# A fused cross-attention and Fourier FFN kernel: copies of weights on other engines or through score banks, a mask and norms ahead of reciprocals, transposes inside a chain

## The chip, the cores and the metric

The kernel runs on one core of a Trainium2 chip. A core has five engines with queues of their own that run in the order in which the program issues to each: TensorE (PE, matrix products and transposes, with weight loads shown apart as PEld), VectorE (DVE), ScalarE (ACT), GpSimd (POOL) and SyncE (SP, here only a queue that starts DMAs). They meet through semaphores. The metric is the device time of one execution in microseconds. The time before is a median over three runs; the profile is one further execution.

## The reference

The inputs are x (2 x 2048 x 512), an encoder context (2 x 128 x 512), and a mask that is 0 for valid keys and 1 for padded ones; all is float32.

```
xn    = layernorm(x)
q,k,v = xn @ wq + bq, ctx @ wk + bk, ctx @ wv + bv          # 16 heads of 32
score = (q k^T / sqrt(32)) * mask;  score = -1e9 where score == 0
x     = x + concat(softmax(score) v) @ wo + bo
x     = x + real(ifft(fft(layernorm(x)) @ (w_re + i w_im))) + bias
```

The FFN's transforms and its weight are all linear, so the kernel works out one real 512 x 512 matrix first (m_ffn), from DFT tables that come in as constants, and the FFN of a row is then one product with it.

## The kernel before, in words

The 4096 rows are cut into eight groups of 512 (i = 0 to 7), each into four tiles of 128 rows (t = 0 to 3). One pass (i, t) computes the scores of one tile against the 128 keys for 16 heads, as two halves w[0] and w[1] of eight heads; `begin(i, t)` issues the 32 score matmuls. Each half goes through four steps of class `Softmax`:

- `masked`: DVE multiplies the scores, in PSUM, with the mask (L345);
- `maxima`: DVE turns zeros into the large negative value and takes a minimum per head (L352, L354, L355);
- `exponentials`: ACT, eight activations with their sums (L361);
- `divided`: DVE takes a reciprocal of the sums (L373) and POOL multiplies by it (L374).

`transposed_weights(i, t, first, end, eng, banks)` then turns the heads' weights on PE, four heads to a bank of PSUM (tpw, L391), and copies the bank to SBUF (pt), on DVE (L396) or ACT (L398). Each bank needs both halves of its tile. Four such banks make a tile, and they are issued as two pairs.

Around the passes other work is laid out by hand. Order in the source is order in each engine's queue. For each group: rows come in by DMA; `relative` subtracts the row's first element (L244, mostly on POOL), `query_statistics` has DVE's statistics (L219, L220) and two POOL steps for the inverse deviation (L223, L224), `query_norm` normalises on DVE (L227), and `query_transposes` turns the tile on PE (tp_a, L194) with a copy on ACT (L196). `Queries` is a chain of matmuls with the query weight and an eviction with the bias, on ACT (L307) or DVE (L309). `context` multiplies turned weights with the values (c, L413), `Project` with wo (o, evicted by DVE into the residual rows, L450). Then the FFN follows: `ffn_statistics`, `ffn_norm` (norm_f on DVE, L227, and then on POOL the addition of the FFN's bias to the residual, L469), `ffn_transposes` (tp_f) and `Ffn` (y, L210 by way of `chain`, evicted by DVE, L514, and stored by DMA). `chain` can call other work between its second and third contraction chunk.

Passes of group 0 and the first two of group 1 are written out one by one, since the making of m_ffn lies between them: `First` (chains h, eviction on ACT L669, sums on POOL L677 and L679 in `first`, and on DVE L690 and L691 in `second`) and `Mirrored` (m, L722, evicted by ACT L732 and L738, finished on POOL L739 and L740). From pass (1, 2) on the function `slot` issues a pass. It takes three chains and lists of further work, called at fixed places: `on_a` follows the mask of the second half, `on_m` its maxima, `on_b` the reciprocal of the first half and the eviction of the second chain, `on_c` the end. Work in the list `carried` is called in the next slot, just behind the first half's mask. The last two groups have lists of their own.

PSUM is held in three pools of two: ps_sc (score tiles of two banks), ps_tp (transposes, one bank) and ps_mm (chains, one bank). A tile waits for the readers of the tile that had its place.

Of the kernel before, what the change touches and what calls it, by code (L numbers as in the profile page):

```python
# [9 lines left out]
FP = mybir.dt.float32  # L10
# [4 lines left out]
P = 128  # L15
# [7 lines left out]
def kernel(  # L23
# [34 lines left out]
    nc = tc.nc  # L58

    B, S, D = x.shape  # L60
    K = enc.shape[1]
    DH = 32
    H = D // DH
    NC = D // P
    NR = P // DH
    HH = H // 2
    TG = 4
# [8 lines left out]
    ps_sc = ctx.enter_context(  # L76
        tc.tile_pool(name="ps_sc", bufs=2, space=bass.MemoryType.PSUM)
    )
# [7 lines left out]
    HC = NC // 2  # L86
# [113 lines left out]
    def call(work):  # L200
        for f, *args in work:
            f(*args)
# [31 lines left out]
    def relative(i, t, eng):  # L234


        xt = rows[i][t]
        d = work.tile([P, D], FP, tag="rel", bufs=4, name=f"rel_{i}_{t}")
        if eng is nc.scalar:
            less = small.tile([P, 1], FP, tag="less", name=f"less_{i}_{t}")  # L240
            nc.scalar.mul(less, xt[:, 0:1], -1.0)
            nc.scalar.activation(d, xt, AF.Identity, bias=less)
        else:
            eng.tensor_scalar(d, xt, xt[:, 0:1], None, ALU.subtract)  # L244
        rels.setdefault(i, []).append(d)
# [15 lines left out]
    def query_statistics(i, first, end):  # L261
        if first == 0:
            mv = small.tile([P, TG, 2], FP, tag="mv", name=f"mv_{i}")
            rstd = small.tile([P, TG], FP, tag="rstd", name=f"rstd_{i}")
            stats[i] = mv, rstd
        mv, rstd = stats[i]
        for t in range(first, end):
            statistics(rels[i][t], mv[:, t, :], f"a{i}_{t}")
        if i == 0:
            inverse_deviations(rstd[:, first:end], mv[:, first:end, 1])  # L270
        elif end == TG:
            inverse_deviations(rstd, mv[:, :, 1])

    def query_norm(i, t):
        mv, rstd = stats[i]
        normalize(rels[i][t], rels[i][t], mv[:, t, :], rstd[:, t : t + 1])

    def query_transposes(i, t):
        if t == 0:
            xnTs[i] = big_tile("xnT", 1, f"xnT_{i}")  # L280
        transpose_rows(
            xnTs[i][:, :, t * P : (t + 1) * P], rels[i][t], f"a{i}_{t}", nc.scalar
        )

    class Queries:
# [5 lines left out]
        def pe(self):  # L291
            i, g = self.i, self.g
            if i not in qTs:
                qTs[i] = big_tile("qT", 2, f"qT_{i}")
            self.ps = chain(
                f"q_{i}_{g}",
                lambda c: wq[:, c, g * P : (g + 1) * P],
                lambda c: xnTs[i][:, c, self.first * P :],
                width=GQ - self.first * P,
                spare=self.spare,  # L300
            )
# [76 lines left out]
    pts = {}  # L378

    def transposed_weights(i, t, first, end, eng=None, banks=None):  # L380
        if t == 0 and first == 0:
            pts[i] = [big_tile("pt", 6, f"pt_{i}_{g}") for g in range(NC)]
        ws = weights[i, t]
        for g in range(first, end):
            ps = (
                banks[g]
                if banks
                else ps_tp.tile([P, NR, P], FP, tag="tp", name=f"tpw_{i}_{t}_{g}")
            )
            for r in range(NR):  # L390
                nc.tensor.transpose(  # L391
                    ps[:, r, :], ws[r // 2].w[:, (r % 2) * NC + g, :], ident
                )
            dst = pts[i][g][:, :, t * P : (t + 1) * P]
            if eng:
                eng.tensor_copy(dst, ps)  # L396
            else:
                nc.scalar.copy(dst, ps)  # L398


    cTs = {}
# [231 lines left out]
    class First:  # L633
# [8 lines left out]
            else:  # L642
                self.lhs = [lambda c, t=t: t[:, c, HD + g :: HC] for t in (wi, wr)]

        def pe(self):
            ps = self.ps = ps_mm.tile([P, D], FP, tag="mm", name=self.name)
            at = 0


            for k, table, odd, n in (  # L650
                (0, cosines, 0, QD + 1),
                (0, cosines, 1, QD),
                (1, sines, 0, QD - 1),
                (1, sines, 1, QD),
            ):
                for b in range(2):
                    c = b * HC + odd
                    nc.tensor.matmul(
                        ps[:, at : at + n],
                        self.lhs[k](c),  # L660
                        table[:, c, :n],
                        start=(b == 0),
                        stop=(b == 1),
                    )
                at += n

        def evict(self):
            self.t = work.tile([P, D], FP, tag="parts", name=f"t_{self.name}")
# [73 lines left out]
    carried = []  # L742

    def run(job):
        job.pe()
        job.evict()
# [115 lines left out]
    h = [First(what, g) for what in range(2) for g in range(HC)]  # L862
    m = [Mirrored(f"m_{g}", half_of(g), m_ffn[:, g, :]) for g in range(NC)]
    rest = [Queries(0, g, 1, g >= HC) for g in range(NC)]
    q = [Queries(1, g) for g in range(NC)]
    values = [Values(b) for b in range(B)]

    w = begin(0, 0)
# [22 lines left out]
    w = begin(0, 1)  # L891
    w[0].masked()
    query_transposes(1, 0)
    query_transposes(1, 1)
    for t in range(TG):
        relative(2, t, nc.gpsimd)
    w[0].maxima()
    values[1].pe(between=[(query_transposes, 1, 2), (query_transposes, 1, 3)])
# [6 lines left out]
    w[1].exponentials()  # L905
    h[0].evict()
    w[0].divided()
    q[0].pe()
    transposed_weights(0, 0, HC, NC)
    q[0].evict()  # L910
    query_statistics(2, 0, TG)
    w[1].divided()
    h[0].first()

    load_rows(3)
    w = begin(0, 2)
# [16 lines left out]
    q = [Queries(2, g) for g in range(NC)]  # L933
    w = begin(0, 3)
    w[0].masked()
    query_transposes(2, 0)
    query_transposes(2, 1)
    h[1].pe()
    query_transposes(2, 2)
    query_transposes(2, 3)  # L940
    h[1].evict()
    w[0].maxima()
    h[0].second()
# [25 lines left out]
    w = begin(1, 0)  # L969
# [6 lines left out]
    relative(3, 3, nc.gpsimd)  # L976
    m[1].pe()
    m[1].evict(add[:, 1:2])
    w[0].exponentials()
    w[1].masked()  # L980
    transposed_weights(0, 3, 0, HC, nc.vector)
    w[1].maxima()
    w[0].divided()
    m[2].pe()
# [10 lines left out]
    w = begin(1, 1)  # L995
# [7 lines left out]
    w[0].exponentials()  # L1003
    w[1].masked()
    q[2].evict()
    transposed_weights(1, 0, 0, HC, nc.vector)
    w[1].maxima()
    run(q[3])
    transposed_weights(1, 0, HC, NC)
    w[1].exponentials()  # L1010
    query_norm(3, 0)
    query_norm(3, 1)
    w[0].divided()
    w[1].divided()


    for i in range(1, last - 1):
        p, pp, n, nn = i - 1, i - 2, i + 1, i + 2
        q = [Queries(n, g) for g in range(NC)]
        q_nn = Queries(nn, 0)  # L1020
        o = [Project(p, t) for t in range(TG)]
        f_p = Ffn(p, 0)
        if i > 1:
            load_rows(nn)
            load_mask(n)
            load_residual(p)
            f_pp = [Ffn(pp, t) for t in range(TG)]
            slot(
                i,
                0,  # L1030
                [f_pp[1], f_pp[2], q[1]],
                turned=(p, TG - 1),
                early=[(ffn_transposes, pp, 2)],
                pool=[(relative, nn, t, nc.gpsimd) for t in range(TG)],
                on_b=[(ffn_norm, pp, 3), (query_statistics, nn, 0, 2)],
                on_c=[(query_statistics, nn, 2, TG)],
                end=[(context, p, 0, 2)],
            )
            slot(
                i,  # L1040
                1,
                [q[2], q[3], f_pp[3]],
                turned=(i, 0),
                early=[(context, p, 2, NC), (ffn_transposes, pp, 3)],
                pool=[(output_bias, p)],
                on_b=[(query_norm, nn, 0), (query_norm, nn, 1)],
            )
        slot(
            i,
            2,  # L1050
            o[:3],
            turned=(i, 1),
            early=[(query_transposes, nn, 0), (query_transposes, nn, 1)],
            on_a=[(ffn_statistics, p, 0)],
            on_b=[(ffn_norm, p, 0), (query_norm, nn, 2), (query_norm, nn, 3)],
            on_c=[(ffn_statistics, p, 1)],
            end=[(ffn_transposes, p, 0)],
        )
        slot(
            i,  # L1060
            3,
            [o[3], f_p, q_nn],
            turned=(i, 2),
            early=[(query_transposes, nn, 2), (query_transposes, nn, 3)],
            on_a=[(ffn_statistics, p, 2)],
            on_b=[(ffn_norm, p, 1), (ffn_statistics, p, 3)],
            on_c=[(ffn_norm, p, 2)],
            end=[(ffn_transposes, p, 1)],
        )
# [4 lines left out]
    i, n, p, pp = last - 1, last, last - 2, last - 3  # L1074
    load_mask(n)
    load_residual(p)
    q = [Queries(n, g) for g in range(NC)]
# [9 lines left out]
        on_b=[(ffn_norm, pp, 3)],  # L1087
        end=[(context, p, 0, 2)],
# [16 lines left out]
        on_b=[(ffn_statistics, p, 0)],  # L1105
# [9 lines left out]
        on_b=[(ffn_norm, p, 1), (ffn_statistics, p, 2), (ffn_statistics, p, 3)],  # L1115
        end=[(ffn_transposes, p, 1)],
    )
    i, p, pp = last, last - 1, last - 2
# [14 lines left out]
    w = begin(i, 1)  # L1133
# [19 lines left out]
    w = begin(i, 2)  # L1153
# [22 lines left out]
    w = begin(i, 3)  # L1176
# [93 lines left out]
```

## Time and profile before

| What | Before |
|---|---|
| median of 3 runs | 535.35 us (534.28 to 536.14) |
| the profiled execution | 534.98 us |
| its span, first to last instruction | 533.0 us |
| DMA over the span | 36.49 MB, mean 68 GB/s |
| granted TensorE clock | 1.000 |

The first two are device times; the span is what the trace covers of the profiled one, so 1.98 us lie around it. In a page's row of an engine stand its busy time, its share of the span and its instructions. In a row of the timeline stand start, length, engine, line, operation, tiles, shapes and a count of like instructions in a row; a bracket tells how long the engine was idle before it, and who ended that.

### The profile page before, as it was taken

How to read it: one execution, taken by the hardware profiler on the slowest of the kernel's cores; microseconds unless marked ns; L12 is line 12 of the kernel's file. 1: busy time of each engine (PE TensorE's matmuls, PEld its weight loads, DVE VectorE, ACT ScalarE, POOL GpSimd, SP SyncE). 2: the span in 40 equal slices, each digit the busy share in tenths (PEclk: the TensorE clock that was granted, in tenths of full speed). 3: DMA queues.
4: the chain of work that ended last, by engine and by line, in shares of the span. 5: the costliest groups of instructions: out<-in, count | busy, mean ns of one | idle time of the engine just before them, and what ended most of it. 6: DMA issues, size and time to landing. Idle time of an engine off the chain costs nothing.

```text
span 533.0 us, 8813 instructions
## 1 busy us (share of the span) xinstructions
PE 522.4 (98%) x3028; PEld 293.3 (55%) x3028; DVE 440.6 (83%) x621; ACT 337.5 (63%) x1286; POOL 336.8 (63%) x276
## 2 busy tenths in 40 slices
PE   8999998998999999999999999999999999999997
PEld 7756675554545555455545555455545555455444
DVE  4788799879987998889987999879867899898351
ACT  3367777476677676666677766666686677766210
POOL 2779469844895459735895459825754466856450
PEclk9999999999999999999999999999999999999999
DMA  9962020000610024000510015000311101301102
GB/s 311 387 231 79 1 88 13 1 1 1 199 41 1 21 73 165 1 20 1 198 41 0 22 42 196 1 22 0 119 41 41 59 0 61 100 0 42 39 0 80
DMA packets 22892, 36.49 MB, mean 68 GB/s; under 512 B 2104, under 2 KB 7488, under 8 KB 22848
## 3 DMA queue, kind: packets, MB, share of 16 engines
q1 hardware_dynamic: 22160, 34.75, 18.9%
q10 hardware_dynamic: 688, 1.18, 0.6%
q8 instruction: 24, 0.39, 0.3%
q14 instruction: 20, 0.16, 0.1%
HBM read 27.53 MB, written 8.39 MB: 67 GB/s over the span
## 4 chain that ended last, share of the span: by engine, by line
PE 74%; DVE 17%; ACT 4%; issue 2%; POOL 1%; DMA 1%; SPq 0%; ACTq 0%; POOLq 0%; DVEq 0%
PE y L210 16%; PE q L210 16%; PE o L210 14%; PE tpw L391 7%; PE c L413 5%; PE sc L326 5%; DVE w L352 4%; ACT w L361 3%; DVE nmax L354 3%; DVE w L345 3%; PE tp_f L194 2%; PE tp_a L194 2%; PE k L558 1%; DVE norm_f L227 1%; PE v L210 1%
## 5 line engine op out<-in xcount | busy, mean ns | idle before, releaser
L361 ACT ACTIVATE w<-w,nmax 128x128 f32<-128x128 f32 x512 | 198.3, 395 | 18.9 <-DVE nmax L355 16.6
L374 POOL TENSOR_TENSOR w<-w,rden 128x1024 f32<-128x1024 f32 x62 | 119.3, 1924 | 74.1 <-DVE rden L373 56.6
L210 PE MATMUL o<-wo,cT 128*128 128x512 f32 x256 | 115.3, 594 | 0.0
L210 PE MATMUL y<-m_ffn,nT 128*128 128x512 f32 x248 | 112.1, 594 | 0.6 <-DVE x L514 0.6
L210 PE MATMUL q<-xnT,wq 128*128 128x512 f32 (+1 forms) x256 | 111.6, 580 | 0.0
L361 ACT ACTIVATION_READ_ACCUMULATOR w<-w,nmax 128x1 f32 x512 | 99.2, 194 | 0.0
L398 ACT COPY pt<-tpw 128x512 f32<-128x512 f32 x112 | 59.8, 586 | 54.9 <-PE tpw L391 54.8
L352 DVE SCALAR_TENSOR_TENSOR w<-w 128x1024 f32<-128x1024 f32 x64 | 88.1, 1377 | 0.8
L345 DVE TENSOR_TENSOR w<-sc,mask 128x1024 f32<-128x1024 f32 x64 | 77.4, 1211 | 12.9 <-PE sc L326 12.2
L354 DVE TENSOR_REDUCE nmax<-w 128x8 f32<-128x1024 f32 x64 | 78.1, 1220 | 2.2
L391 PEld LDWEIGHTS tpw<-ident,w 128*128 128x128 f32 x496 | 57.6, 141 | 35.3 <-issue 29.4
L210 PEld LDWEIGHTS o<-wo,cT 128*128 128x128 f32 x256 | 46.2, 190 | 47.5 <-issue 46.1
L210 PEld LDWEIGHTS q<-xnT,wq 128*128 128x128 f32 x256 | 46.4, 190 | 44.6 <-issue 40.2
L210 PEld LDWEIGHTS y<-m_ffn,nT 128*128 128x128 f32 x248 | 44.5, 190 | 45.2 <-issue 44.2
L391 PE MATMUL tpw<-ident,w 128*128 128x128 f32 x496 | 65.4, 274 | 2.8 <-DVE pt L396 1.4
L469 POOL TENSOR_TENSOR x<-x,bf 128x512 f32<-128x512 f32 x32 | 50.5, 1579 | 19.0 <-DVE norm_f L227 19.0
L223 POOL TENSOR_SCALAR rstd_f<-mv_f 128x1 f32<-128x1 f32 x32 | 18.2, 570 | 65.1 <-DVE mv_f L220 65.1
L429 POOL TENSOR_TENSOR x<-x,bo 128x512 f32<-128x512 f32 x32 | 48.4, 1542 | 0.0
L244 POOL TENSOR_SCALAR rel<-rows 128x512 f32<-128x512 f32 x26 | 44.7, 1731 | 1.3 <-PE tp_a L194 1.3
L373 DVE RECIPROCAL rden<-den 128x8 f32<-128x8 f32 x64 | 12.6, 197 | 33.0 <-ACT w L361 32.8
L326 PEld LDWEIGHTS sc<-kT,qT 32*128 32x128 f32 x1024 | 31.5, 186 | 14.1 <-issue 13.2
L196 ACT COPY nT<-tp_f 128x512 f32<-128x512 f32 x29 | 16.9, 583 | 34.1 <-PE tp_f L194 33.9
(92 smaller groups left out, 558.6 us busy)
## 6 DMA issues: line engine op xcount, KB each, us to landing
rows<-in_x_dram SPq DMA_DIRECT2D x32, 256.0 KB, 4.2
x<-in_x_dram SPq DMA_DIRECT2D x32, 256.0 KB, 5.0
out_dram<-x SPq DMA_DIRECT2D x31, 256.0 KB, 2.0
mask<-in_mask_Bx1xSxS_fk_dram SPq DMA_DIRECT2D x8, 256.0 KB, 4.4
wk<-in_L_xattn_wk_w_dram ACTq DMA_DIRECT2D x2, 512.0 KB, 7.1
wq<-in_L_xattn_wq_w_dram SPq DMA_DIRECT2D x1, 1024.0 KB, 6.8
wr<-n_L_ffn_w_freq_real_dram SPq DMA_DIRECT2D x2, 512.0 KB
wi<-n_L_ffn_w_freq_imag_dram SPq DMA_DIRECT2D x2, 512.0 KB, 9.0
```

Of the source, the lines that this page charges most:

```text
L210: nc.tensor.matmul(ps, lhs(c), rhs(c), start=(c == 0), stop=(c == NC - 1))
L244: eng.tensor_scalar(d, xt, xt[:, 0:1], None, ALU.subtract)
L326: nc.tensor.matmul(sc[r // 2][:, r % 2, g, :], qTs[i][rows, g, t * P : (t + 1) * P], kT[rows, g, b * K : (b + 1) * K], start=True, stop=True,)
L345: nc.vector.tensor_tensor(self.w, self.sc.rearrange("p r g k -> p (r g) k"), self.mrow, ALU.mult)
L352: nc.vector.scalar_tensor_tensor(w, w, 0.0, w, ALU.is_equal, ALU.subtract)
L354: nc.vector.tensor_reduce(self.nmax, w, AX.X, ALU.min)
L361: nc.scalar.activation(w[:, h, :], w[:, h, :], AF.Exp, bias=self.nmax[:, h : h + 1], scale=-UNIT, accum_out=self.den[:, h : h + 1],)
L374: eng.tensor_tensor(w, w, rden.unsqueeze(2).to_broadcast([P, HH, K]), ALU.mult)
L391: nc.tensor.transpose(ps[:, r, :], ws[r // 2].w[:, (r % 2) * NC + g, :], ident)
L398: nc.scalar.copy(dst, ps)
L429: nc.gpsimd.tensor_tensor(xs[:, t, :], xs[:, t, :], bo, ALU.add)
L469: nc.gpsimd.tensor_tensor(xt, xt, bf, ALU.add)
```

## The change

- `transposed_weights`, where banks are handed to it, issues all its transposes first and then its copies.
- `First.pe` can call other work between its first and its second half; in pass (0, 3), two query transposes of group 2 move there, from behind the chain.
- `relative(2, 3)` moves from POOL in pass (0, 1) to DVE behind the first half's reciprocal of the same pass; the statistics of that tile, and with them the inverse deviation of the group, move behind the second half's division.
- In pass (1, 0), the first two copies of (0, 3)'s weights move from DVE, behind the second half's mask, to ACT, ahead of the first half's exponentials.
- In pass (1, 1), the first two banks of (1, 0)'s weights are the two of a score tile; the other two banks follow at once, ahead of chain q[3]; q[3] is evicted behind the second half's exponentials; and the second half's division is carried into the slot of pass (1, 2), behind that slot's first mask.
- In the slots of t = 2 of groups 1 to 5, three norms move from `on_b` to `on_m`.

```diff
@@ transposed_weights
         ws = weights[i, t]
+        def copy(g, ps):
+            dst = pts[i][g][:, :, t * P : (t + 1) * P]
+            if eng:
+                eng.tensor_copy(dst, ps)
+            else:
+                nc.scalar.copy(dst, ps)
         for g in range(first, end):
...
-            dst = pts[i][g][:, :, t * P : (t + 1) * P]
-            if eng:
-                eng.tensor_copy(dst, ps)
-            else:
-                nc.scalar.copy(dst, ps)
+            if not banks:
+                copy(g, ps)
+        if banks:
+            for g in range(first, end):
+                copy(g, banks[g])
@@ First
-        def pe(self):
+        def pe(self, between=()):
...
                 at += n
+                if at == D // 2 + 1:
+                    call(between)
@@ pass (0, 1)
-    for t in range(TG):
+    for t in range(TG - 1):
         relative(2, t, nc.gpsimd)
...
     w[0].divided()
+    relative(2, TG - 1, nc.vector)
     q[0].pe()
     transposed_weights(0, 0, HC, NC)
     q[0].evict()
-    query_statistics(2, 0, TG)
+    query_statistics(2, 0, TG - 1)
     w[1].divided()
+    query_statistics(2, TG - 1, TG)
     h[0].first()
@@ pass (0, 3)
     query_transposes(2, 1)
-    h[1].pe()
-    query_transposes(2, 2)
-    query_transposes(2, 3)
+    h[1].pe(between=[(query_transposes, 2, 2), (query_transposes, 2, 3)])
     h[1].evict()
@@ pass (1, 0)
     m[1].evict(add[:, 1:2])
+    transposed_weights(0, 3, 0, HC)
     w[0].exponentials()
     w[1].masked()
-    transposed_weights(0, 3, 0, HC, nc.vector)
     w[1].maxima()
@@ pass (1, 1)
     q[2].evict()
-    transposed_weights(1, 0, 0, HC, nc.vector)
+    free = ps_sc.tile([P, 2, NC, K], FP, tag="sc", name="tpw_1_0")
+    transposed_weights(1, 0, 0, HC, nc.vector, [free[:, g] for g in range(HC)])
+    transposed_weights(1, 0, HC, NC)
     w[1].maxima()
-    run(q[3])
-    transposed_weights(1, 0, HC, NC)
+    q[3].pe()
     w[1].exponentials()
+    q[3].evict()
     query_norm(3, 0)
     query_norm(3, 1)
     w[0].divided()
-    w[1].divided()
+    carried.append(w[1].divided)
@@ for i in range(1, last - 1): slot t = 2
-            on_b=[(ffn_norm, p, 0), (query_norm, nn, 2), (query_norm, nn, 3)],
+            on_m=[(ffn_norm, p, 0), (query_norm, nn, 2), (query_norm, nn, 3)],
```

## The prediction

> **What bounds the kernel now.** I read the page's busy shares first, then the table of busy time by stretches (one stretch per pass of scores), then the waits, then each engine's timeline around every wait of TensorE. The page:
>
> ```profile
> PE 522.4 (98%) x3028; PEld 293.3 (55%) x3028; DVE 440.6 (83%) x621; ACT 337.5 (63%) x1286; POOL 336.8 (63%) x276
> ```
>
> ```profile
> 63.50:78.00 14.50, 14.17 (x136) 11.70 (x132) 13.12 (x20) 10.71 (x43) 8.66 (x14) 1.00 0.21 75
> 78.00:93.60 15.60, 14.22 (x101) 8.79 (x101) 14.86 (x22) 10.17 (x43) 15.44 (x12) 1.00 0.06 17
> ...
> 107.00:124.00 17.00, 14.88 (x88) 8.21 (x86) 13.85 (x20) 12.99 (x57) 8.16 (x6) 1.00 0.00 1
> ...
> 199.10:396.60 197.50, 197.50 (x1153) 105.71 (x1152) 171.44 (x231) 137.32 (x521) 130.09 (x97) 1.00 0.18 60
> ```
>
> In the stretches the columns are length, then PE, PEld, DVE, ACT and POOL busy. From 199 to 397 us PE never pauses, so an edit that acts only there can win nothing. The early groups have holes, and the waits of 34 to 125 us name their causes (total, times, longest):
>
> ```profile
> PE tp_f L194 <- DVE norm_f L227: 1.7, 1, 1.7
> ...
> PE tpw L391 <- DVE pt L396: 1.4, 1, 1.4
> ...
> PE tpw L391 <- POOL w L374: 0.9, 2, 0.5
> ...
> PE tpw L391 <- ACT xnT L196: 0.3, 1, 0.3
> ```
>
> These idle times leave out the modelled tail of the matmul before, so I measure from start to start in PE's timeline (start, length, instructions):
>
> ```profile
> 53.73 0.38 PE L391 MATMUL tpw<-ident,w 128*128 128x128 f32 x2
> 54.59 0.87 PE L391 MATMUL tpw<-ident,w 128*128 128x128 f32 x6 [0.48 <-POOL w L374]
> ...
> 67.06 1.04 PE L194 MATMUL tp_a<-ident,rel 128*128 128x128 f32 x8
> 68.42 1.06 PE L391 MATMUL tpw<-ident,w 128*128 128x128 f32 x8 [0.33 <-ACT xnT L196]
> ...
> 83.39 1.90 PE L722 MATMUL m<-dft,half 128*128 128x257 f32 x8
> 86.67 1.25 PE L391 MATMUL tpw<-ident,w 128*128 128x128 f32 x8 [1.38 <-DVE pt L396]
> ...
> 112.17 0.38 PE L391 MATMUL tpw<-ident,w 128*128 128x128 f32 x2
> 112.99 0.87 PE L391 MATMUL tpw<-ident,w 128*128 128x128 f32 x6 [0.44 <-POOL w L374]
> ...
> 118.01 3.60 PE L210 MATMUL o<-wo,cT 128*128 128x512 f32 x8
> 123.28 0.63 PE L194 MATMUL tp_f<-ident,norm_f 128*128 128x128 f32 x4 [1.67 <-DVE norm_f L227]
> ```
>
> Unhindered, a transpose starts every 0.109 us, an m matmul every 0.216, a 512-column matmul every 0.430. So the five holes are 54.59-53.95 = 0.64; 68.42-67.93 = 0.49; 86.67-85.12 = 1.55; 112.99-112.39 = 0.60; 123.28-121.45 = 1.83: in all 5.11 us. Each lies where the change edits. That is the most it can win, about 1%.
>
> A rule is weighed here. The Trainium skill, "Perfetto Trace Analysis", section "Identifying the Most-Contended Engine", calls matmul busy time a poor measure of distance from the roofline and takes the share of weight loading. The row has 98% and 55%. By the page's rule 45% of the span might be open; by the start-to-start steps, what waits cost is 5.11 us here. The steps decide, since the change removes no matmul.
>
> **The change part by part** (times on the clock of before, unless called new).
>
> *relative(2,3), POOL to DVE.* It takes 1.81 us (a quarter of 7.24) off POOL ahead of w0's division in pass (0,1), and adds 0.49 (the DVE row of L244) to DVE. One pair of statistics (0.66+0.18) moves behind w1's reciprocal, POOL's two rstd steps (0.23+1.04) behind w1's division. SP's fourth row load of group 3 is released 2 us sooner. POOL's three remaining steps end near 46.7, w0's division (1.89) at 48.6; w1's exponentials end at 48.74, its division at about 50.9 instead of 54.54. PE asks at 53.95: **0.64 won**. On DVE the addition fills an idle 0.54 that waited for POOL's fourth step; without that cover the next mask (50.29) is 0.4 late, and the normalisations at 59.4 to 61.3 have 2 us until PE's transposes at 64.24.
> Here a rule speaks against the edit: the Trainium skill, "SBUF — State Buffer", section "Who interferes with whom", has DVE's two-port instructions and GpSimd block each other for a whole instruction. The trace agrees: norm_f took 0.50 alone and 1.85 beside a POOL division. By the free row relative costs 0.49, by the blocked one 1.85. The latter puts w1's division at 52.2, still ahead of 53.95: the sum is the same.
>
> *h[1] with two transposes inside.* Nothing is added. The chain's 16 matmuls take 1.89 (65.17 to 67.06); its second half (0.94) moves behind the transposes and covers the ACT copies (67.69 to 68.77) that the weight transposes waited for. The new transposes ask for their banks at 66.11; the copies of the first two end about 65.6 and 66.1. **0.49 won**. ACT's eviction of h[1] is behind the copies, at about 68.2 instead of 68.65, so exponentials are not later.
>
> *The copies of (0,3), DVE to ACT.* Two copies (1.27) leave DVE, two of 0.58 join ACT ahead of w0's exponentials, in an idle 1.47 there (waiting for nmax). Without that cover the exponentials are 1.07 late, w0's division 1.1, which has over 6 us until its transposes. The hole of **1.55 closes**: the banks are free a microsecond before PE asks. What is late next: q[1]'s eviction on DVE (91.39, behind two statistics) frees the bank of the second context product, at 92.20 now with nothing to spare. PE would be 2.68 early there, DVE by its own queue about 2.4 (1.27 of copies; 1.1 from half.second, L691, which spent 2.12 instead of 0.41 beside a POOL division that now starts 1.1 sooner). I charge **0.3 back**; the bounds are 0 and, if L691's part does not come, 0.9.
>
> *Pass (1,1): two copies through a score bank, q[3] behind the transposes, its eviction behind w1's exponentials.* Same instructions. The bank's owner was masked 4 us before; the next scores (106.70) need the DVE copies out (103.35): 3.3 us. w1's exponentials started 107.46, behind q[3]'s eviction and two copies, although nmax was there at 106.76: now 0.66 earlier. q[3]'s eviction ends at 110.6 instead of 106.6; its bank is asked for at 113.70 (o[1]), its queries by the next group's scores at 138.5. Then the *mask of (1,2) ahead of w1's reciprocal*: 1.17 in an idle 2.91; scores end at 107.80, so the mask ends at 109.1, before the exponentials (109.9): the reciprocal waits for nothing new. Without the idle time it would be 1.17 late, and w1's division and PE with it. w1's division ends 112.25 instead of 112.94; PE asks at 112.39. Of 0.60 I take **0.55**; bounds 0 and 0.60. Free besides: later DVE work of this pass is 1.2 earlier.
>
> *Three norms ahead of reciprocals, five passes.* In (1,2) norm_f stood behind o[1]'s eviction, then took 1.85 beside w0's division. New: right after nmax (120.71), rstd ready at 120.01, POOL idle: 0.50, so 121.25 at worst, PE asks at 121.45. **1.83 won**; bounds 1.0 (if blocked once) and 1.83. In the other four passes norm_f ends at 183.1, PE asks at 183.89: nothing to win. Cost: POOL's bias addition (1.5) goes ahead of w0's division, and blocks one norm. Reciprocal of w0: 180.6 to 183.1 (0.55 for norm_f, 1.95 for the pair as its row has it); w0's division to 185.3, w1's to 187.2 (187.13 before). PE asks at 190.1; o[1]'s bank, freed at 183.9 instead of 181.3, is asked for at 186.45. Covered by 2.5 to 2.9 us; beyond that PE waits one for one.
>
> *The split loop* changes nothing at the end of the kernel, where each call has one bank.
>
> **Sum**: 0.64+0.49+1.55-0.3+0.55+1.83 = 4.76. Behind it PE is unbroken to 397, so it stays. The profiled execution had 534.98 (span 533.0 and 1.98 around it), giving 530.2, span 528.2. It lies 0.37 under the median of 535.35 (runs 534.28 to 536.14); with a third of that for the median: **530.4**.
>
> **Rivals.** *DVE keeps the pace from 64 to 100 us.* It is busy 14.86 of 15.60 there, and the copies taken away shorten it by 1.27 alone; L691's gain fails, PE waits for q[1]'s eviction and (1,1) gives half. Won: 0.64+1.2+0.2+1.1 = 3.1, or 531.9. Against it: DVE waits 1.18 for PE at 102. *The time comes back later.* PE arrives 4.8 us early at 124 us, and loads or POOL (15.72 busy of 15.80 in 138.5 to 154.3) don't: about 534.6. Against it: no DMA wait stands in the stretches after 124, and PE is unbroken there while POOL waits for DVE. *Slower: the bias addition and the port.* In five passes w1's division slips, and the transposes of the next pass wait. It decides once the division is over 2.9 us late; a net loss of 1.6 needs 6.4 in all, 1.3 a pass, hence a slip of 4.2: time 536.6 to 538. For it: blocked norms of 1.85 each. Against it: at that place POOL has only the one addition to block with.
>
> **How the numbers follow.** A measurement here tells about 0.3% (1.6 us) from no change. Forecast (529.7 to 531.3): 0.62. DVE's pace (531.3 to 533.2): 0.19. Comes back: 0.10. Slower: 0.07; the rest is small gains. Range 529.2 to 533.3: the floor is all 5.11 and the scatter of runs, the ceiling takes in the first rival. Faster 0.82, same 0.10, slower 0.08.
>
> **What would show it.** Right: the five holes under 0.15 us each, PE's scores of (1,3) near 118.9 instead of 123.84, span near 528.2, at most one hole of 0.5 before the second context product near 89.5. Wrong: tpw of any pass t=3 waiting for POOL, a hole over 0.5 there, or scores of (1,3) early but the end not.

## The result: 532.46 us, 0.4% faster, and half of the forecast gain

| | before | changed |
|---|---|---|
| median | 534.63 us (534.28 to 536.14, 7 runs) | 532.46 us (532.10 to 533.75, 7 runs) |
| ratio, 95% interval | | 0.996 (0.9949 to 0.997) |
| profiled execution | 534.98 us | 532.30 us |
| its span | 533.0 us | 530.2 us |
| granted TensorE clock | 1.000 | 1.000 |

The kernel became 2.2 us faster, where 4.76 was the forecast. The time lies inside the prediction's range (529.2 to 533.3), but above the window that it held for likeliest (529.7 to 531.3); it falls in the window of its first rival, DVE's pace (531.3 to 533.2). Busy shares hardly move. The page of the changed kernel:

```profile
PE 521.7 (98%) x3028; PEld 293.7 (55%) x3028; DVE 433.9 (82%) x620; ACT 338.3 (64%) x1288; POOL 338.1 (64%) x275
```

The gain has to be placed pass by pass. A pass is taken from the start of its first score matmul to that of the next pass, which needs no model of where a matmul ends:

| pass | before | changed | difference | forecast |
|---|---|---|---|---|
| (0,2), holds the transposes of (0,1) | 14.05 | 13.35 | -0.70 | -0.64 |
| (0,3), transposes in chain h[1] | 14.36 | 13.84 | -0.52 | -0.49 |
| (1,0), copies of (0,3) | 15.70 | 15.29 | -0.41 | -1.25 |
| (1,1) | 13.50 | 13.50 | 0 | 0 |
| (1,2), mask and norms | 17.14 | 16.45 | -0.69 | -2.38 |
| (1,3) | 14.62 | 14.62 | 0 | 0 |
| together | 89.36 | 87.05 | -2.31 | -4.76 |

From the scores of (2,0) to the end both spans have 394.55 us (533.01-138.45 = 394.56, and 530.20-135.65), so all of it lies in these passes. (The two spans differ by 2.81; the other 0.49 is the head of the kernel up to the scores of (0,2), which varied from 48.41 to 49.58 us over all the profiles taken for this study, whatever was edited.) Two passes fall short, (1,0) and (1,2). The stretches of the changed kernel for (1,0), (1,2) and the steady part (length, then PE, PEld, DVE, ACT, POOL busy):

```profile
75.79:91.08 15.29, 14.31 (x99) 8.97 (x98) 14.56 (x20) 11.60 (x48) 15.13 (x11) 1.00 0.06 18
...
104.58:121.03 16.45, 14.89 (x86) 8.41 (x85) 14.32 (x22) 13.01 (x55) 10.07 (x7) 1.00 0.00 1
...
196.30:393.70 197.40, 197.40 (x1149) 105.65 (x1148) 167.24 (x231) 137.32 (x521) 130.13 (x97) 1.00 0.17 60
```

PE has no hole in the steady part, as forecast. In (1,0) it is busy 14.31 of 15.29 and DVE 14.56, in (1,2) 14.89 of 16.45. The waits from 34 to 125 us (total, times, longest) say on whom:

```profile
PE tpw L399 <- POOL w L374: 1.0, 1, 1.0
PE c L421 <- DVE qT L309: 1.0, 1, 1.0
...
PE tp_a L194 <- DVE rel L227: 0.5, 1, 0.5
```

None of the four kinds of wait that stood in this list before is left as it was: three are gone, POOL's division has one wait for two, and two new waits came. In PE's timeline (L399 is the old L391, L421 the old L413):

```profile
83.66 1.04 PE L399 MATMUL tpw<-ident,w 128*128 128x128 f32 x8
...
88.06 1.07 PE L421 MATMUL c<-pt,v 128*32 128x512 f32 x8
90.08 1.07 PE L421 MATMUL c<-pt,v 128*32 128x512 f32 x8 [0.95 <-DVE qT L309]
...
106.28 1.08 PE L194 MATMUL tp_a<-ident,rel 128*128 128x128 f32 x8 [0.53 <-DVE rel L227]
...
112.04 0.88 PE L399 MATMUL tpw<-ident,w 128*128 128x128 f32 x6 [1.02 <-POOL w L374]
...
120.50 0.60 PE L194 MATMUL tp_f<-ident,norm_f 128*128 128x128 f32 x4
```

The first row and the last are the places of the two largest old holes, 1.55 and 1.83, now without a bracket; those of 0.64 and 0.49 are closed too (the transposes start at 53.24 and 66.74, eight in a row). What is left is three holes: 90.08-88.06-0.91 = 1.11 (the next eight context matmuls could start 0.91 after these; sixteen in one row, in e3 below, take 1.98), 106.28-105.68 = 0.60 (what follows the scores could start 1.10 after their start at 104.58), and 112.04-110.86 = 1.18 (two transposes started at 110.64, by 0.109 each). They sum to 2.89, where 5.11 stood before: 2.22 less, close to the measured gain of 2.17.

DVE's rows behind these holes, POOL's beside them, and one of ACT's:

```profile
70.86 1.21 DVE L352 SCALAR_TENSOR_TENSOR w<-w 128x1024 f32<-128x1024 f32 x1
...
75.73 2.12 DVE L701 TENSOR_TENSOR half<-u_half 128x254 f32<-128x254 f32 x1
...
84.86 1.40 DVE L352 SCALAR_TENSOR_TENSOR w<-w 128x1024 f32<-128x1024 f32 x1
...
89.31 0.72 DVE L309 TENSOR_SCALAR qT<-q,bq 128x512 f32<-128x512 f32 x1
...
94.72 2.30 DVE L352 SCALAR_TENSOR_TENSOR w<-w 128x1024 f32<-128x1024 f32 x1
...
104.58 1.10 DVE L355 TENSOR_SCALAR nmax<-nmax 128x8 f32<-128x8 f32 x1
...
109.06 1.17 DVE L352 SCALAR_TENSOR_TENSOR w<-w 128x1024 f32<-128x1024 f32 x1
110.27 1.22 DVE L354 TENSOR_REDUCE nmax<-w 128x8 f32<-128x1024 f32 x1
```

```profile
71.18 1.43 POOL L687 TENSOR_TENSOR u_half<-t_half 128x254 f32<-128x254 f32 x1 [1.73 <-ACT t_half L679]
...
75.47 2.10 POOL L374 TENSOR_TENSOR w<-w,rden 128x1024 f32<-128x1024 f32 x1
...
94.05 1.90 POOL L374 TENSOR_TENSOR w<-w,rden 128x1024 f32<-128x1024 f32 x1
...
99.69 5.97 POOL L437 TENSOR_TENSOR x<-x,bo 128x512 f32<-128x512 f32 x4
...
109.29 2.70 POOL L374 TENSOR_TENSOR w<-w,rden 128x1024 f32<-128x1024 f32 x1 [0.55 <-DVE rden L373]
```

```profile
105.72 0.40 ACT L361 ACTIVATE w<-w,nmax 128x128 f32<-128x128 f32 x1 [2.01 <-DVE nmax L355]
```

The kernel before had in these places, on DVE, POOL and ACT (L677 and L691 are the new L687 and L701):

```profile
76.92 2.12 DVE L691 TENSOR_TENSOR half<-u_half 128x254 f32<-128x254 f32 x1
...
87.13 1.21 DVE L352 SCALAR_TENSOR_TENSOR w<-w 128x1024 f32<-128x1024 f32 x1
```

```profile
72.89 0.92 POOL L677 TENSOR_TENSOR u_half<-t_half 128x254 f32<-128x254 f32 x1 [1.89 <-ACT t_half L669]
...
76.66 2.10 POOL L374 TENSOR_TENSOR w<-w,rden 128x1024 f32<-128x1024 f32 x1
...
111.04 1.90 POOL L374 TENSOR_TENSOR w<-w,rden 128x1024 f32<-128x1024 f32 x1 [1.22 <-DVE rden L373]
```

```profile
107.46 0.42 ACT L361 ACTIVATE w<-w,nmax 128x128 f32<-128x128 f32 x1
```

The same instructions take two lengths: L701 0.41 or 2.12, L352 1.17 or 2.30, L355 0.17 or 1.10, the division 1.90 or 2.70. The long ones stand beside an instruction of the other of the two engines: L352 of 94.72 beside the division of 94.05, L355 of 104.58 beside the last of the four bias additions (which end at 105.68 and 105.66). The one that started second pays: L701 started 0.26 behind the division and ended 0.28 after its end (77.85 and 77.57); at 109.06 L352 started first, kept its 1.17, and the division took 0.80 more. That is the rule of the Trainium skill's page "SBUF — State Buffer", section "Who interferes with whom", by which the first to issue keeps the shared port pair for its whole instruction. Not every DVE instruction is slowed: L354 took 1.22 inside the long division of 109.29, and between 1.219 and 1.222 in all its 64 executions. None of these rows has a bracket of idle time for it: a stall of this kind is counted as busy. (The 0.55 at 109.29 is the division's wait for its reciprocal.)

### The profile page after: what moved, and what is told of

It reads as the page before. It is cut to its first block, busy times and chain, and to the rows that moved or that the text cites. A ratio compares the mean times of both kernels' runs of the same rounds, so it can differ in the third digit from the quotient of the medians.

```text
span 530.2 us, 8808 instructions
## 1 busy us (share of the span) xinstructions
PE 521.7 (98%) x3028; PEld 293.7 (55%) x3028; DVE 433.9 (82%) x620; ACT 338.3 (64%) x1288; POOL 338.1 (64%) x275
## 3 DMA queue, kind: packets, MB, share of 16 engines
q10 hardware_dynamic: 688, 1.18, 0.6%
## 4 chain that ended last, share of the span: by engine, by line
PE 78%; DVE 15%; ACT 3%; POOL 2%; issue 1%; POOLq 0%; ACTq 0%; DVEq 0%
PE q L210 17%; PE y L210 16%; PE o L210 16%; PE tpw L399 8%; PE c L421 5%; PE sc L326 5%; DVE w L352 3%; DVE nmax L354 3%; ACT w L361 3%; DVE w L345 3%; PE tp_a L194 3%; PE tp_f L194 2%; PE k L566 1%; PE v L210 1%; DVE norm_f L227 1%
## 5 line engine op out<-in xcount | busy, mean ns | idle before, releaser
L390 ACT COPY pt<-tpw 128x512 f32<-128x512 f32 x114 | 60.9, 586 | 55.5 <-PE tpw L399 55.4
L345 DVE TENSOR_TENSOR w<-sc,mask 128x1024 f32<-128x1024 f32 x64 | 77.6, 1213 | 14.2 <-PE sc L326 12.2
L352 DVE SCALAR_TENSOR_TENSOR w<-w 128x1024 f32<-128x1024 f32 x64 | 86.7, 1355 | 0.8
L354 DVE TENSOR_REDUCE nmax<-w 128x8 f32<-128x1024 f32 x64 | 78.1, 1220 | 2.2
L399 PEld LDWEIGHTS tpw<-ident,w 128*128 128x128 f32 x496 | 57.7, 141 | 32.5 <-issue 29.1
L399 PE MATMUL tpw<-ident,w 128*128 128x128 f32 x496 | 65.0, 273 | 1.2 <-POOL w L374 1.0
```

The lines of the kernel that those rows point to most:

```text
L345: nc.vector.tensor_tensor(self.w, self.sc.rearrange("p r g k -> p (r g) k"), self.mrow, ALU.mult)
L352: nc.vector.scalar_tensor_tensor(w, w, 0.0, w, ALU.is_equal, ALU.subtract)
L354: nc.vector.tensor_reduce(self.nmax, w, AX.X, ALU.min)
L399: nc.tensor.transpose(ps[:, r, :], ws[r // 2].w[:, (r % 2) * NC + g, :], ident)
```

## The experiments

The theory: from about 63 to 122 us DVE's queue sets PE's pace, its own work and the time in which POOL blocks it together. PE's old holes were places where that queue was late; closing one moves the wait to the next thing that PE needs from DVE, unless DVE or POOL loses work. (From 64 to 106 us DVE is busy 39.86 of 42.00 in the changed kernel; behind that its reciprocals also wait for ACT.) The rivals: each hole has a local cause (one division, one bank), or the norms' new place is what went wrong; and POOL was busy 15.13 of the 15.29 us of (1,0), so its own queue could be the limit there. Pass lengths of all kernels, in the order of the table above:

| kernel | (0,2) | (0,3) | (1,0) | (1,1) | (1,2) | (1,3) | sum |
|---|---|---|---|---|---|---|---|
| before | 14.05 | 14.36 | 15.70 | 13.50 | 17.14 | 14.62 | 89.36 |
| changed | 13.35 | 13.84 | 15.29 | 13.50 | 16.45 | 14.62 | 87.05 |
| e1 | 13.35 | 13.83 | 15.29 | 13.50 | 15.64 | 15.84 | 87.46 |
| e2 | 13.35 | 13.84 | 15.31 | 13.50 | 16.44 | 14.62 | 87.06 |
| e3 | 13.35 | 13.84 | 14.21 | 13.50 | 17.53 | 14.62 | 87.04 |
| e4 | 13.35 | 13.84 | 15.30 | 13.50 | 15.03 | 14.62 | 85.65 |
| e5 | 14.32 | 14.36 | 15.70 | 13.50 | 15.27 | 15.84 | 89.00 |
| e6 | 13.74 | 14.11 | 14.67 | 13.50 | 17.31 | 14.62 | 87.95 |
| e7 | 13.35 | 13.83 | 15.26 | 13.50 | 15.42 | 14.62 | 85.99 |
| e8 | 14.49 | 14.35 | 14.78 | 13.50 | 17.48 | 14.62 | 89.23 |
| e9 | 13.35 | 13.84 | 15.22 | 13.50 | 15.02 | 14.62 | 85.55 |
| e10 | 13.35 | 13.97 | 14.62 | 13.54 | 15.03 | 14.62 | 85.12 |

Pass (0,2) varies by half a microsecond in code that is the same up to there (14.05, 14.32, 14.49 in before, e5 and e8; 13.74 in e6 and 13.35 in the other eight), so it isn't used to judge an experiment, and the 0.70 that the change wins there is rough. All times are medians, with the ratio to the kernel before in the same set of runs.

### e1: the division not carried past the mask

In the changed kernel, pass (1,1):

```diff
-    carried.append(w[1].divided)
+    w[1].divided()
```

> The changed kernel, with the second half's division of pass (1,1) issued at the end of that pass again, ahead of the mask of (1,2). Port theory: in the changed kernel the mask went ahead, so the division (109.29) met L352 of the first half on DVE (109.06) and took 2.70 instead of 1.90; PE waited 1.19 for it. With the order of before, the division runs beside the mask and takes 1.9, PE's hole shrinks from 1.19 to about 0.35, and the time falls by about 0.8 us against the changed kernel (about 2.9 under before). The reading of the prediction (the mask fills idle time and the division is not later for it): the hole stays 1.2 or grows by the mask's 1.17, and the time is the same or up to 1.2 us more than the changed kernel's.

Measured: 532.59 us against 534.79, ratio 0.9954 (0.9941 to 0.9966): no different from the changed kernel as a whole, where 0.8 less had been expected. POOL at the division, PE there and in the next pass, and ACT:

```profile
109.25 1.90 POOL L374 TENSOR_TENSOR w<-w,rden 128x1024 f32<-128x1024 f32 x1 [0.55 <-DVE rden L373]
```

```profile
110.60 0.38 PE L399 MATMUL tpw<-ident,w 128*128 128x128 f32 x2
111.21 0.87 PE L399 MATMUL tpw<-ident,w 128*128 128x128 f32 x6 [0.23 <-POOL w L374]
...
122.76 0.66 PE L194 MATMUL tp_a<-ident,rel 128*128 128x128 f32 x4 [0.81 <-ACT nT L196]
```

```profile
119.05 0.40 ACT L361 ACTIVATE w<-w,nmax 128x128 f32<-128x128 f32 x1 [1.18 <-DVE nmax L355]
```

The division starts at the same time and takes 1.90 for 2.70; its hole shrinks from 1.18 to 0.39, and (1,2) from 16.45 to 15.64. So in the changed kernel the mask's going first made the reciprocal no earlier, and it brought the mask's successor L352 beside the division: where a gain was forecast, 0.8 was lost in that pass. But (1,3) takes 1.22 more here. The mask stands behind the reciprocal again, L352 behind it now comes second beside the division and takes 2.00 (at 110.23), and the exponentials of (1,2)'s second half start at 119.05, late for nmax. The copy of the turned norm stands behind them in ACT's queue, and the transposes wait for its bank. The mask's going first is what keeps (1,3) at 14.62: the prediction had it as "later DVE work of this pass is 1.2 earlier", and counted nothing for it. Both passes together, the mask's place wins 0.41; the times, 532.46 and 532.59, can't tell.

### e2: the norms back behind the eviction

```diff
-            on_m=[(ffn_norm, p, 0), (query_norm, nn, 2), (query_norm, nn, 3)],
+            on_b=[(ffn_norm, p, 0), (query_norm, nn, 2), (query_norm, nn, 3)],
```

> The changed kernel, with the three norms of the slots of t = 2 behind the reciprocal again. The prediction's sum: the hole ahead of tp_f in (1,2) returns, 1.83 us, so the time is about that of before minus 0.4. Rival: the mask of (1,2) that now goes first has pulled DVE's queue forward by itself, and PE comes 0.6 later to that place because of the larger hole at the weights; norm_f then ends near 119.9 with PE asking at 120.5, the hole stays closed, and the time stays within 0.3 us of the changed kernel (about 2.2 under before).

Measured: 532.34 us against 534.79, ratio 0.9955 (0.9941 to 0.9968), and the same passes as the changed kernel to 0.02. DVE, then PE:

```profile
117.66 1.85 DVE L227 TENSOR_SCALAR norm_f<-x,mv_f,rstd_f 128x512 f32<-128x512 f32 x1
```

```profile
120.32 0.60 PE L194 MATMUL tp_f<-ident,norm_f 128*128 128x128 f32 x4
```

The norm is as slow as before (1.85), but with the other edits in place DVE reaches it earlier, and it ends at 119.5, before PE asks. The norms' move is then worth nothing, in this pass and in the four later ones.

### e3: two statistics behind q[1]'s eviction

In the changed kernel, pass (1,0):

```diff
-    query_statistics(3, 0, 2)
     q[1].pe()
     q[1].evict(nc.vector)
     context(0, 0, 2, nc.vector)
+    query_statistics(3, 0, 2)
     w[1].divided()
```

> The changed kernel, with DVE's statistics of (3,0) and (3,1) behind q[1]'s eviction and the two context copies. Local theory: the hole of 1.1 us ahead of the second context product is the two statistics (1.6) queued ahead of the eviction; it closes, and the time falls by 1.1 us. Pace theory: DVE has no idle time left between 64 and 106 us, so the hole closes at 90 and comes back at the next place where PE needs DVE (tp_a behind the norms near 106, or the weights near 112); the time falls by 0.3 us or less.

Measured: 532.55 us against 534.79, ratio 0.9954 (0.9940 to 0.9968). (1,0) becomes 1.08 shorter and (1,2) 1.08 longer. PE:

```profile
88.46 1.98 PE L421 MATMUL c<-pt,v 128*32 128x512 f32 x16
...
106.65 1.08 PE L194 MATMUL tp_a<-ident,rel 128*128 128x128 f32 x8 [1.60 <-DVE rel L227]
```

The sixteen context matmuls run as one, so the hole of 1.11 is gone; the transposes of the norms then wait 1.60 where they had waited 0.53. DVE does the same work in another order and reaches its norms at the same time. This is the case for the pace, and against a local cause of the hole in (1,0).

### e4: without the output bias of group 0

The kernel leaves out `output_bias(0)`, the four additions on POOL in pass (1,1).

```diff
     m[3].evict(add[:, 3:4])
-    output_bias(0)
     w[0].maxima()
```

> The changed kernel without the four POOL additions of the output bias to group 0's rows (that group's output lacks the bias). Port theory: these additions (99.7 to 105.7) are what lengthens DVE's L352 and L355 in pass (1,1) (2.30 for 1.2, 1.71 for 1.2, 0.64 and 1.10 for 0.17, so about 2.5 us together); without them DVE is 2 us earlier at 106, the holes at tp_a (0.6) and at the weights (1.19) close or fall under 0.4, and the time falls by 1.4 to 1.8 us. If instead DVE's own sum of work sets these places, the holes stay and the time changes by less than 0.4 us.

Measured: 530.75 us against 534.79, ratio 0.9924 (0.9909 to 0.9938). (1,2) becomes 1.42 shorter, and no later pass gives it back. DVE, then PE:

```profile
103.99 0.17 DVE L355 TENSOR_SCALAR nmax<-nmax 128x8 f32<-128x8 f32 x1
```

```profile
105.58 1.09 PE L194 MATMUL tp_a<-ident,rel 128*128 128x128 f32 x8
...
109.95 0.38 PE L399 MATMUL tpw<-ident,w 128*128 128x128 f32 x2
110.52 0.87 PE L399 MATMUL tpw<-ident,w 128*128 128x128 f32 x6 [0.19 <-POOL w L374]
```

```profile
107.77 2.70 POOL L374 TENSOR_TENSOR w<-w,rden 128x1024 f32<-128x1024 f32 x1 [0.55 <-DVE rden L373]
```

Work taken from POOL, an engine that is idle over 6 us of the 16.45 of this pass, makes DVE's instructions short again (L355 0.17 for 1.10, the L352 before it 1.22 for 1.71), and PE's hole of 0.60 before the norms' transposes closes. The hole at the weights falls from 1.18 to 0.35, although the division takes 2.70 here too: nmax is ready earlier, and the exponentials of (1,1)'s second half start 0.29 ahead of the scores of (1,2), at 104.19, where they had started 1.14 behind them. That is what POOL costs here: the time that it blocks DVE, not its queue.

### e5: the norms alone

The kernel before with the norms' edit and nothing else:

```diff
-            on_b=[(ffn_norm, p, 0), (query_norm, nn, 2), (query_norm, nn, 3)],
+            on_m=[(ffn_norm, p, 0), (query_norm, nn, 2), (query_norm, nn, 3)],
```

> The kernel before with the three norms of the slots of t = 2 moved to on_m, and nothing else. The prediction's term: the hole of 1.83 us ahead of tp_f in (1,2) closes, pass (1,2) falls from 17.14 to about 15.3 us, the time by 1.8 us; other passes stay. If instead the norms are a matter of DVE's queue as a whole (rival: what they gain at tp_f is given back at the next transposes of queries in (1,3)), pass (1,2) falls and pass (1,3) grows by as much, and the time stays within 0.5 us of before.

Measured: 534.76 us against 535.29, ratio 0.9988 (0.9982 to 0.9995). (1,2) becomes 1.87 shorter, as the prediction had it to 0.04, and (1,3) 1.22 longer. PE, and ACT's copy:

```profile
125.02 0.66 PE L194 MATMUL tp_a<-ident,rel 128*128 128x128 f32 x4 [0.81 <-ACT nT L196]
```

```profile
124.41 0.56 ACT L196 COPY nT<-tp_f 128x512 f32<-128x512 f32 x1
```

It is the wait of e1: PE comes early, and the bank that it wants next is emptied by ACT behind its exponentials. The old hole had hidden that. By the passes 0.65 is kept, and by the times 0.53.

### e6: the division behind the second sums

In the changed kernel, pass (0,3); one subtraction of group 3 moves with the division:

```diff
-    w[0].divided()
-    relative(3, 0, nc.gpsimd)
     h[2].second()
     h[3].second()
+    w[0].divided()
...
     w[1].divided()
+    relative(3, 0, nc.gpsimd)
```

> The changed kernel, in pass (0,3) with the first half's division (its reciprocal and its POOL product) behind the last second of h[3], and relative(3,0) behind the second half's division. Port theory for pass (1,0): L701 (2.12 us instead of 0.41) loses the port because POOL's division is queued right behind the sums that L701 waits for, so both always start together; with the division behind it L701 takes 0.41, DVE is about 1.7 us earlier at 78, q[1]'s eviction comes in time, and pass (1,0) falls from 15.29 to 14.2 us. Whether that stays: if DVE's whole queue was the pace, the later holes of pass (1,2) shrink or stay, and the time falls by about 1.1 us; if POOL's bias additions set pass (1,2), that pass grows by about 1.1 as it did with the statistics moved, and the time stays.

Measured: 533.25 us against 535.29, ratio 0.9959 (0.9947 to 0.9971). DVE, then POOL:

```profile
77.55 0.42 DVE L701 TENSOR_TENSOR half<-u_half 128x254 f32<-128x254 f32 x1
...
80.57 2.48 DVE L352 SCALAR_TENSOR_TENSOR w<-w 128x1024 f32<-128x1024 f32 x1
```

```profile
78.22 3.75 POOL L374 TENSOR_TENSOR w<-w,rden 128x1024 f32<-128x1024 f32 x2 [0.89 <-PE sc L326]
```

L701 takes 0.42 for 2.12, so the division beside it was the cause. But the two divisions now run back to back and block L352, which takes 2.48. (1,0) falls to 14.67 and not to the 14.2 expected; (0,3) becomes 0.27 longer and (1,2) 0.86: given back again, as in e3.

### e7: group 3's relative on ACT

In the changed kernel, four subtractions leave POOL:

```diff
     w[0].divided()
-    relative(3, 0, nc.gpsimd)
...
     run(q[0])
+    relative(3, 0, nc.scalar)
...
-    relative(3, 1, nc.gpsimd)
...
     m[0].evict(add[:, 0:1])
+    relative(3, 1, nc.scalar)
     w[0].maxima()
-    relative(3, 2, nc.gpsimd)
-    relative(3, 3, nc.gpsimd)
...
     transposed_weights(0, 3, 0, HC)
+    relative(3, 2, nc.scalar)
...
     w[1].exponentials()
+    relative(3, 3, nc.scalar)
     query_statistics(3, 0, 2)
```

> The changed kernel with all four steps relative(3,t) on ACT (0.19 and 0.72 us each there) in its idle times instead of POOL (1.74 to 2.53 each). Port theory: POOL then blocks DVE less in pass (1,0) (L352 1.96 and 1.40 instead of 1.2), DVE is about 1 us earlier at q[1]'s eviction, pass (1,0) falls by 0.8 to 1.1 us; the bias additions keep their place behind m[3] (98 us), so pass (1,2) keeps its holes or gives the gain back, and the time falls by 0 to 1 us. Pace theory without the port (only DVE's own work counts): no change, within 0.3 us.

Measured: 531.88 us against 535.29, ratio 0.9937 (0.9925 to 0.9949). DVE:

```profile
95.30 1.22 DVE L352 SCALAR_TENSOR_TENSOR w<-w 128x1024 f32<-128x1024 f32 x1
```

POOL:

```profile
92.73 1.90 POOL L374 TENSOR_TENSOR w<-w,rden 128x1024 f32<-128x1024 f32 x1 [0.81 <-DVE rden L373]
...
98.94 5.96 POOL L437 TENSOR_TENSOR x<-x,bo 128x512 f32<-128x512 f32 x4
```

The expectation for (1,0) failed: it stays at 15.26. L701 still takes 2.12, and the two L352 of that pass 2.00 and 1.34, for POOL's divisions and its sums for m_ffn are still beside them. POOL is busy 10.50 us of this pass, where it was 15.13 of 15.29, and PE's hole is nearly the same (1.05): so POOL's own queue was not what made (1,0) long. The gain is in (1,2), 1.03. In the changed kernel the second division of (1,0) came late in POOL's queue, at 94.05, and L352 of (1,1) met it; here it starts at 92.73 and is over before L352 starts at 95.30, which takes 1.22 for 2.30. The additions end at 104.90, ahead of L355 (105.06, 0.17), and the norms are there when PE asks for them. That a lighter POOL is not given back was foreseen; where it would show was not.

### e8: the copies alone

The kernel before, with the copies of (0,3) on ACT and nothing else:

```diff
     m[1].evict(add[:, 1:2])
+    transposed_weights(0, 3, 0, HC)
     w[0].exponentials()
     w[1].masked()
-    transposed_weights(0, 3, 0, HC, nc.vector)
     w[1].maxima()
```

> The kernel before with only the first two copies of the weights of (0,3) on ACT, ahead of the exponentials of (1,0). The prediction's sum for this part: hole of 1.55 closed, 0.3 back at the second context product, pass (1,0) 15.70 to 14.45 us, time 1.25 us under before. The pace theory: with PE less far ahead than in the whole change, q[1]'s eviction is just in time (DVE is 1.27 of copies earlier, PE 1.55), pass (1,0) falls by about 1.3, and since DVE is earlier at the later places too, pass (1,2) stays at 17.1; the time falls by about 1.3 us, more than the 0.41 that the pass won in the whole change.

Measured: 534.72 us against 535.29, ratio 0.9991 (0.9984 to 0.9999). (1,0) becomes 0.92 shorter and (1,2) 0.34 longer, and the time falls by 0.57. The pace theory had expected 1.3 kept in full, and the prediction's sum 1.25: neither came. PE:

```profile
107.84 1.08 PE L194 MATMUL tp_a<-ident,rel 128*128 128x128 f32 x8 [0.49 <-DVE rel L227]
```

Without the mask's and the norms' edits (the old hole of 1.84 at tp_f stays) the same new wait for the norms appears that the changed kernel has, so it comes of PE's being early, not of those edits.

### e9: the output bias in four places

e7, with `output_bias(0)` cut into four calls of one tile each, one ahead of the second division of (0,3), two in (1,0), the last in (1,1):

```diff
+    output_bias(0, 0, 1)
     w[1].divided()
...
     m[1].evict(add[:, 1:2])
+    output_bias(0, 1, 2)
...
     query_statistics(3, 2, TG)
+    output_bias(0, 2, 3)
...
     m[3].evict(add[:, 3:4])
-    output_bias(0)
+    output_bias(0, 3, 4)
```

> The kernel with relative(3,t) on ACT, and the four bias additions of group 0 spread: one ahead of the second half's division of (0,3), one behind m[1], one at the end of (1,0), one behind m[3], where DVE by the trace works from PSUM or with one SBUF operand. Port theory: pass (1,1) and (1,2) lose most of their blocked DVE time (1.3 us in pass (1,2) and the 1.2 of the mid pass), so the pass (1,2) falls from 15.42 to about 15.0, as it did with the additions left out (15.03); time 0.4 us under the version with relatives on ACT alone, 1 us under the changed kernel. If an addition meets a division or L352 in its new place instead, pass (1,0) grows by 0.5 or more and the time does not fall.

Measured: 532.05 us against 535.34, ratio 0.9937 (0.9923 to 0.9950). The passes of the profile are 0.44 shorter than e7's, with (1,2) at 15.02, the length of e4 where the additions were left out. In the time that isn't resolved from e7: the medians are 532.05 and 531.88, and the profiled execution was the fastest of e9's five, 531.12.

### e10: both, and the statistics behind

e9 and the edit of e3 together.

> The same with the statistics of (3,0) and (3,1) behind q[1]'s eviction and the context copies, which in the changed kernel moved 1.08 us from pass (1,0) to pass (1,2) and won nothing. If DVE's blocked time was what made pass (1,2) give it back, now that POOL is out of the way pass (1,0) falls to 14.2 and pass (1,2) grows by 0.5 at most: time 0.6 to 1 us under the version without it. If DVE's own work is the limit there even unblocked, (1,2) grows by 1.1 again and the time stays.

Measured: 530.73 us against 535.34, ratio 0.9914 (0.9901 to 0.9928): 4.6 us, the fastest version that leaves nothing out, and its interval lies wholly below that of the changed kernel (0.9949 to 0.997). PE:

```profile
82.08 0.38 PE L399 MATMUL tpw<-ident,w 128*128 128x128 f32 x2
82.76 0.87 PE L399 MATMUL tpw<-ident,w 128*128 128x128 f32 x6 [0.29 <-POOL w L374]
...
89.61 1.98 PE L421 MATMUL c<-pt,v 128*32 128x512 f32 x16
...
106.16 1.09 PE L194 MATMUL tp_a<-ident,rel 128*128 128x128 f32 x8
```

The edit that e3 gave back in full now takes 0.60 off (1,0), 15.22 to 14.62, and (1,2) stays at 15.03. (A new hole of 0.46 in (1,0), at 82.76, takes a part, and (0,3) is 0.13 longer.) Against e9 alone the gain isn't resolved in the time, since the runs overlap (530.15 to 531.44, and 531.12 to 532.43); it rests on the passes, 0.43 in all. What differs from e3 is that POOL's blocking has left the stretch behind: the two L352 of (1,1) take 1.22 and 1.21, where the changed kernel had 2.30 and 1.71. So the reading is that DVE's queue now has the slack to be reordered.

## Why the prediction was half right

**Right.** The three holes at 54.59, 68.42 and 86.67 us closed by what was to close them, at 0.64, 0.49 and 1.55 (passes (0,2) and (0,3) became 0.70 and 0.52 shorter, the first of them rough; no run takes the edits behind these two one by one). The steady part was unbroken, the tail equal, and the bias additions ahead of the divisions in five passes cost nothing. The rule on the shared port had been weighed for relative on DVE, which took 0.81 and cost PE nothing, for L691 and for the norms. It had not been weighed for the instructions that decided the two terms that failed. Of the prediction's own signs, four of the five holes closed; the scores of (1,3) came at 121.03 and not near 118.9, and the hole before the second context product was 1.11 where at most 0.5 was allowed.

**The step "about 2.4 by its own queue" of the copies: 0.3 back was 1.11.** Count both kernels from their scores of (0,2), at 49.09 and 48.60. PE could ask for the second context product 2.73 earlier than before, as the sum had it (2.68). But DVE started q[1]'s eviction only 1.59 earlier (42.30 and 40.71), where 2.4 was counted: that is the miss, 0.8. Half of it lies in the 1.1 for L691. L691 (now L701) waits for POOL's sums, and the division is the next instruction in POOL's queue behind those sums; so the two start together in both kernels, 0.26 apart, with 2.12 spent each time. They could only move as a pair, and they moved by 0.70, because one of POOL's sums started behind DVE's L352 and took 1.43 for 0.92 (71.18 and 72.89). The other half lies in the 1.27 of the copies, of which 0.89 came: the L352 behind them now stood beside POOL and took 1.40 for 1.21 (84.86 and 87.13), and part of the copies' time had overlapped with their neighbours. e6 takes the division away and L701 falls to 0.42. The measured 1.11 lies even beyond the prediction's bound of 0.9; in e8, with the copies alone, it is 0.85. The first rival had this step, and its 531.9 is nearest to the measured 532.5.

**The step of the mask in (1,1) and (1,2): 0.55 won was 0.58 lost.** PE's hole at the weights went from 0.60 to 1.18, for two reasons. The sum had the exponentials, and so the reciprocal and the division, 0.7 earlier. They waited for nmax: the exponentials started 1.14 behind the scores of (1,2) (105.72-104.58), where before it was 0.76 (107.46-106.70). L352 and L355 had stood beside the 5.97 us of bias additions; in e4, without these, the hole is 0.35. And the sum took the division's duration as unchanged. It started at 109.29; L352, which follows the mask at once, had started at 109.06, and the division took 2.70; in e1, where 1.90 is enough, the hole is 0.39. The prediction had asked what the mask delays on DVE and not what it brings beside POOL. The same late L352 and L355 made the norms late by 0.60 ahead of it: PE, early, arrived before them. What the mask's place did win, 1.22 in (1,3) by e1, the sum had left out.

**The step of the norms: 1.83 won was right alone, and not additive.** Alone (e5), (1,2) became 1.87 shorter, and 1.22 came back one pass later, at a bank behind ACT's exponentials that the prediction never looked at. (There too the exponentials waited 1.18 for nmax.) With the other edits in place it gives nothing (e2): those had moved the norm ahead of PE's request already.

**The sum.** The five holes were added as if each were independent, and 4.76 was held for the likeliest. Four of the experiments show that in this stretch what reordering wins at one hole comes back, in part or in whole, at the next waits; in pass lengths, +1.08 for -1.08 (e3), +0.86 for -0.62 (e6, with 0.27 more in (0,3)), +1.22 for -1.87 (e5) and +1.22 for -0.81 (e1). e8, which takes work from DVE as well, gives back 0.34 of 0.92. DVE's time spent blocked, the excess over the free durations of the instructions, shows where: in (1,0) and (1,1) it rose from 0.79 and 1.09 before to 1.02 and 2.15, and fell in (1,2) from 3.17 to 2.25. In (1,0) and (1,1) together that is 1.29 more: as much as the 1.27 that the copies had freed on DVE. Most of it is the L352 of 94.72, 2.30 for 1.23: DVE came to it 1.6 earlier than before, POOL's division only 0.03 earlier (both counted from the scores of (0,2)), and so the two met. Not settled is how the terms divide the gain, since the edits were not all taken one by one.

## What to carry to other kernels

By these runs, holes of the engine that bounds the kernel may be added up only if the engine that they wait for has slack between them. Where it had next to none, here from (1,0) on, an edit that reordered work moved the hole in whole or in part, and most of what was kept came of taking work away, or what blocked that work. For every instruction that is moved, look at what it will run beside as well as at what it is queued behind.

## What the runs showed of the hardware

- The blocking is of whole instructions, and tiny ones aren't spared: L355, of 128x8 elements, took 1.10 us beside POOL's additions and 0.17 without them. L352 had 1.17 and 2.30, the norm 0.50 and 1.85, the sums of 128x254 elements 0.42 and 2.12. In the other direction POOL's division took 1.90 alone and 2.70 beside L352. L354, which reads the same 128x1024 elements, took 1.22 in every case.
- The page counts all this as busy. DVE was busy 14.56 us of the 15.29 of pass (1,0), a share that says nothing of the part of it that was blocked; only rows of the same instruction, side by side, tell it.
